# Four chained transformer blocks: attention buffers in four one-batch places, five threads of 1, 1, 2, 2 and 2 batches

## The chip, the cores and the metric

The kernel runs on one core of a Trainium2 chip. The metric is the device time of one execution in microseconds (us), the median of repeated runs. Everything is computed in 32-bit floats. The core's engines are TensorE (PE in the profile, with PEld for its weight loads), VectorE (DVE), ScalarE (ACT), GpSimd (POOL) and SyncE (SP), which here issues DMAs only.

## The reference

Eight batches of 128 tokens with 256 features (x) and a context of the same shape (ctx) pass through four blocks. Attention has 16 heads everywhere. Cut to what matters:

```python
# L0: heads of 16 features, key mask per batch
x = x + attn(ln(x) @ q_w, ctx @ k_w, ctx @ v_w, mask) @ cproj_w
x = x + gelu_tanh(ln(x) @ fc_w) @ proj_w              # 256 -> 1024 -> 256
# L1: keys and values from [ctx, x], so 256 keys; mask on the ctx half
y = attn(x @ q_w, [ctx, x] @ k_w, [ctx, x] @ v_w, mask) @ out_w + x
x = gelu_tanh(rmsnorm(y) @ mlp_w1) @ mlp_w2 + x
# L2: twice, with heads of 128 features and one learned key and value more
for i in (1, 2):
    x = x + attn(ln(x) @ wq, [ctx @ wk, bias_k], [ctx @ wv, bias_v]) @ wo   # 256 -> 2048 -> 256
x = x + gelu(ln(x) @ w_fc1) @ w_fc2
# L3: self-attention, cross-attention, MLP; the masks multiply and shift the scores
q, k, v = split(ln(x) @ w_qkv);  x = x + attn(q, k, v, ltor_mask) @ w_ao
x = x + attn(ln(x) @ w_q, *split(ctx @ w_kv), cross_mask) @ w_co
x = x + gelu_tanh(ln(x) @ w1) @ w2
```

Biases stand on every product, and `ln` has a scale and an offset. The batches do not depend on one another.

## The kernel before

**Threads.** `SIZES` (line 25) splits the eight batches into threads, `(2, 2, 2, 2)`. One thread takes its batches through all four blocks (`blocks`, line 1362). Each thread loads all weights itself through `loader` (line 510): pieces of 512 KB from HBM, up to 4 pieces held per thread and 11 in all (`NW, NWT`). A thread's loader and blocks start when the thread two before it has left block 1 (`front_done`) and the thread three before it has left the wide attention of block 2 (`wide_done`).

**The order of the work** is written by a planner (class `Plan`, line 77 and after) when the program is built. Every piece of work is a generator that asks for buffers (`Slots`), waits for events, and asks for an engine with an urgency. The planner keeps a clock, gives each engine the most urgent piece that is ready, and estimates what the piece lasts with `_weight`. The urgencies are the sum of a number for the kind of work (`U`) and one for the thread's stage (`LATE`). What comes out is a fixed order of instructions per engine; on the chip only data and buffers make an engine wait. Where TensorE has nothing to do[...], the planner issues a matmul of the identity as a filler (`idle_work`, line 397). DMAs are issued by SP in order, in the first microseconds by ACT too.

**Line 333** is where the wrapper of the engines issues every compute instruction, so nearly all rows of the profile name L333, and tile names tell them apart. `mm`, `tl` and `sc` are banks of PSUM: two banks for products, two for small things, and one tile of four banks for scores. `w` is a piece of weights, `hT` the normed activations transposed, `kb` a buffer for MLP activations and for keys and queries of the wide attention, `t` one for scores of the softmax.

**Products.** `proj` (line 541) gives feature-major results: a 128x128 piece of weights is the stationary operand, and the thread's tokens stream (256 columns for two batches). `back` (line 683) gives token-major results: 128 tokens are stationary and 256 columns of weights stream, batch by batch. Each f32 matmul of the program shows as two records in the trace, a transpose as one.

**Small-head attention** (`attention`, line 799) has two cores. `by_keys` (blocks 0 and 1) computes scores twice, once for the maxima, and exponentiates them with keys on the partitions. `by_pairs` (block 3) has queries on the partitions, multiplies and adds the mask on DVE and POOL, exponentiates on ACT, normalizes on POOL, and transposes. `attn_lock` lets two threads hold buffers for keys `k`, values `v`, queries `q`, result `attnT` and `mask`, each with room for two batches.

**Wide attention** (`wide_attention`, line 1163) goes through four groups of four heads, twice. `keys_values` (line 1172) makes a group's keys and values from the context alone, so it may run early: `AHEAD` names the groups that a thread makes before its block 0. The learned value's bias comes through two loads, `bv` and `bb`, and a subtraction on POOL (`value_bias`, line 1289); there are two buffers for `bv` and one for `bb`. `group` (line 1232) makes queries and scores, and `after_scores` (line 1302) the rest.

Of the kernel before, what the change touches and what calls it, by code (L numbers as in the profile page):

```python
# [18 lines left out]
P = 128  # L19
B = 8  # L20
D = 256
# [3 lines left out]
SIZES = (2, 2, 2, 2)  # L25
# [37 lines left out]
AHEAD = [[(1, 0), (1, 1)], [], [], []]  # L63
U = {'take': -0.44, 'taken': -1, 'norm': -0.47, 'mask': 0.26, 'k': 2.41, 'q': 1.79, 'v': 2.5, 'by key': 0.5, 'softmax': 2.46, 'weights': 1.63, 'pairs': 0.75, 'out': 1.79, 'mlp norm': 0.75, 'mlp 1': 4.29, 'mlp 2': 1.92, 'wide norm': -1, 'wide k': 3.49, 'wide q': 4.0, 'wide v': 4.43, 'wide s': 1.19, 'wide': -0.3, 'ahead': 4.34, 'load': -0.39}
LATE = [(1.69, 2.1, 2.22, -0.57, 1.75, 0.04, 2.53, 1.2, 4.53, 1.81), (12.77, 7.95, 10.47, 7.4, 1.7, -1, 8.48, 3.14, 7.46, 6.32), (3.27, 2.62, 3.89, 0.6, 2.14, -1, 4.58, 4.56, 5.62, 0.26), (0.03, 1.69, 0.31, 1.11, 0.24, 3.18, -0.81, -0.64, -0.7, 1.05)]
# [17 lines left out]
class Plan:  # L83
# [12 lines left out]
    def __init__(self):  # L96
        self.now = 0
        self.seq = 0
        self.events = []
        self.asked = []  # L100
        self.until = {e: 0 for e in self.SEEN}
        self.weight, self.shared, self.wrote = 0, False, []
        self.idle_work = None
        self.both_until = {"DVE": 0, "POOL": 0}
        self.clock = Clock()
        self.count = 0
        self.log = []
        self.table = None
        self.dma_until = 0
        self.live = {}  # L110
# [152 lines left out]
def _weight(eng, name, args, kw):  # L263
# [25 lines left out]
    if eng == "DVE":  # L289
# [6 lines left out]
        if n <= 8:  # L296
            return 68, False
# [40 lines left out]
class Engines:  # L338
    def __init__(self, nc, plan):
        self.tensor, self.vector = Engine(nc.tensor, plan, "PE"), Engine(nc.vector, plan, "DVE")  # L340
        self.scalar, self.gpsimd = Engine(nc.scalar, plan, "ACT"), Engine(nc.gpsimd, plan, "POOL")
        self.sync = nc.sync


def op(eng, f, lat=None, table=None):
    return ((eng, 480 if eng == "SP" else 0, f, lat, table),)
# [8 lines left out]
def four_blocks(ctx: ExitStack, tc: tile.TileContext, a: dict, out: bass.AP):  # L355
# [35 lines left out]
    attn_lock, x1_slots = Slots(2), Slots(2)  # L391
    row_slots, bv_slots, bb_slots, w_slots = Slots(2), Slots(2), Slots(1), Slots(NWT)

    def kb():
        return new(act, [P, 2 * P], "kb", bufs=20)

# [15 lines left out]
    def dma(f, kb_, early):  # L412

        yield op("SP", lambda: f(nc.sync)) + (op("ACT", lambda: f(nc.scalar)) if early else ())
# [38 lines left out]
    class Thread:  # L453
        def __init__(self, h, b0, nb):
# [10 lines left out]
            self.late = 0.0  # L465
            self.ahead = {}

# [5 lines left out]
    def weight_list():  # L473
# [22 lines left out]
        for i in (1, 2):  # L496
            for hg in range(4):
# [12 lines left out]
    def loader(T):  # L510
        names = list(weight_list())
        first = {f"l{i}{hg}{x}" for i, hg in AHEAD[T.h] for x in "kv"}
# [23 lines left out]
    def drop(T, n=1):  # L536
        plan.put(T.w_slots, n)
# [47 lines left out]
    def norm(T, src, e, w, b, adds, rows, hT, ready, row_done, urgency):  # L585
# [4 lines left out]
        else:  # L590
# [17 lines left out]
            def root():  # L608
# [11 lines left out]
                if b is not None:  # L620
                    nc.vector.tensor_tensor(z, mean, v, ALU.mult)

# [60 lines left out]
    def back(lhsT, n, w, x, row_in, then):  # L683
# [3 lines left out]
        def part(b, c0):  # L687
            def f(p):
                q = parts(p, nb, D)
                for c in range(c0, min(c0 + 4, n)):  # L690
                    nc.tensor.matmul(
                        q[:, b, :], lhsT=lhsT(c)[:, b * P : (b + 1) * P], rhs=w(c),
# [11 lines left out]
    def product(ops, take):  # L704
# [5 lines left out]
        return spawn(taken(p, take), U["taken"], Plan.SEEN["PE"])  # L710
# [6 lines left out]
    def mlp(T, name, src, e, w, b, b1, func, table, adds, to):  # L717
# [7 lines left out]
        def first():  # L725
            yield (kb_slots, NF)
            for m in range(0, NF, 2):
                hs = [kb(), kb()]
                hid.extend(hs)

                def take(p, m=m, hs=hs):
                    yield from each(*(op("ACT", lambda i=i: nc.scalar.activation(
                        hs[i][:, : T.nt], p[:, i * T.nt : (i + 1) * T.nt], func, bias=col(b1, m + i)), None, table)
                        for i in range(2)))
                hid_in.append((yield from product(
                    proj(T.w[f"{name}1{m // 4}"], hT, (m % 4, m % 4 + 1)), take)))
                if m % 4 == 2:
# [9 lines left out]
        def second():  # L747
            yield from product(*back(lambda c: hid[c], NF, lambda c: T.w[f"{name}2{c // 4}"][:, c % 4, :], to,
                                     row_in, lambda: plan.set(there)))
            drop(T, 2)  # L750
            plan.put(kb_slots, NF)
# [4 lines left out]
    def key_bias(mask, dst, hs, ks, ks_in, name, dtype, T, may_be_none):  # L756
# [5 lines left out]
        raw = mask[:, 0].rearrange("p b k -> p (b k)").bitcast(dtype)[:, : T.nt].rearrange("p (b k) -> p b k", b=nb)  # L762
        m = mask[:, 1]
        ms = new(act, [P, 2, nb], "ms", bufs=2)
        kss = new(act, [P, 2, NC, nb], "kss", bufs=2)
        yield spawn(load(raw, a[name][:, T.tokens].rearrange("o (b k) -> o b k", k=P).partition_broadcast(P), 64 * nb), -1)
        yield ks_in

        def minus():
            nc.vector.tensor_scalar(m, raw, 0.0, -BIG, ALU.is_equal, ALU.mult)  # L770
            some = new(act, [P, nb], "some", bufs=2)
# [5 lines left out]
            for e in range(2):  # L777
                nc.vector.tensor_scalar(hs[:, e], some, half[e], None, ALU.mult)
                nc.vector.tensor_scalar(ms[:, e], some, mask_row[e], None, ALU.mult)
                for c in range(NC):  # L780
                    nc.vector.tensor_scalar(kss[:, e, c], some, ks[:, e, c : c + 1], None, ALU.mult)

        yield op("DVE", minus)
        yield from each(*(
# [14 lines left out]
    def attention(T, name, norm, ns, own_keys, scale, qb, kb_, vb, mask_of, masks, to):  # L799
# [6 lines left out]
        yield (attn_lock, 1)  # L806
        hT, hT_in = yield from normed(T, *norm, U["norm"] + late)
        ready, row_in = T.ready, T.row_in
        mask = new(act, [P, 2, nb, P], "mask", bufs=2)
        hs = new(act, [P, 2, nb], "hs", bufs=2)  # L810
        ne = 2 if by_key else 1
        k = new(act, [P, 2, NC, nb, 2, P], "k", bufs=2)[:, :ne, :, :, :ns]
        v = new(act, [P, 2, nb, 8, 3, 16], "v", bufs=2)[:, :ns]
        q = new(act, [P, 2, NC, nt], "q", bufs=2)
        attnT = new(act, [P, NC, nt], "attnT", bufs=2)
# [64 lines left out]
        def queries():  # L880
            def take(p):
                yield from each(*(either(
                    lambda m=m, e=e: nc.scalar.activation(
                        q[:, e, m, :], p[:, m * nt : (m + 1) * nt], AF.Identity,
                        bias=qs[:, e, m : m + 1], scale=par[e]),
                    lambda m=m, e=e: nc.vector.tensor_scalar(
                        q[:, e, m, :], p[:, m * nt : (m + 1) * nt], par[e], qs[:, e, m : m + 1], ALU.mult, ALU.add),
# [17 lines left out]
        def out():  # L905
            yield from product(*back(lambda c: attnT[:, c, :], NC, lambda c: wo[:, c, :], to,
# [3 lines left out]
            plan.put(attn_lock)  # L910
# [5 lines left out]
    def by_keys(T, ns, scale, mask, masks, q, k, v, v_in, vb, attnT):  # L916
# [4 lines left out]
        def item(b, c0, n):  # L921
            tok = slice(b * P, (b + 1) * P)
# [5 lines left out]
            def by_query():  # L928
                for e in range(2):
                    for c in cs:  # L930
                        j = e * n + c - c0
                        for r in range(4):
                            part = slice(32 * r, 32 * r + 32)
                            nc.tensor.matmul(
                                s[:, r, j * nk : (j + 1) * nk], lhsT=q[part, e, c, tok],
# [25 lines left out]
            to = q[:, :, c0 : c0 + n, tok]  # L961
# [513 lines left out]
```

## Time and profile before

| | |
|---|---|
| median of 3 runs | 1197.38 us (1197.1 to 1198.49) |
| the profiled execution | 1198.46 us |
| its span, first to last instruction | 1196.7 us |
| TensorE busy | 1145.7 us, 8318 records |
| VectorE, ScalarE, GpSimd busy | 751.2, 574.1, 339.1 us |
| moved by DMA | 145.59 MB, mean 122 GB/s |
| matmuls of the identity (mm<-ident) | 92 records, 17.4 us |
| loads of activation tables on ACT | 50, 64.2 us |

How to read it: busy times are unions of an engine's instructions. Matmuls are pipelined; a record of a matmul reaches about 0.17 us into the next one, so the distance from one start to the next is the pace, not the length of a record. The rows of 40 digits cut the span into slices of 30 us. The chain of work that ended last goes back from the last instruction to what released it, step by step.

### The profile page before, as it was taken

What the parts mean: (1) busy time and instruction counts of PE and PEld (TensorE: products, weight loads), DVE (VectorE), ACT (ScalarE), POOL (GpSimd) and SP (SyncE); (2) the same over time, 40 slices, a digit from 0 to 9 for tenths busy, and PEclk for the clock granted to TensorE, in tenths of its full rate; (3) what the DMA queues carried; (4) which work ended last, traced back from release to release, by engine and by line L of the source; (5) the groups of instructions that cost most, each with busy time, mean ns of one, the idle gap of its engine ahead of it and who ended that gap; (6) DMA issues with size and microseconds to landing.
All of it is one profiled execution on the core that took longest, in us unless ns stands there. A gap on an engine that the chain in (4) does not pass through costs nothing.

```text
span 1196.7 us, 21922 instructions
## 1 busy us (share of the span) xinstructions
PE 1145.7 (96%) x8318; PEld 937.0 (78%) x8318; DVE 751.2 (63%) x1943; ACT 574.1 (48%) x1448; POOL 339.1 (28%) x392
## 2 busy tenths in 40 slices
PE   8899889999999999999999999999999999999888
PEld 7577668788887777787888897787887887877767
DVE  7755668744554867977872365626568456778872
ACT  4344544452433345675653243434436334686972
POOL 4021111112221210360611022211217212475870
PEclk9899999999999999999999999999999999999999
DMA  9423131336444324343324644543544543432120
GB/s 319 131 84 116 54 98 58 125 117 191 131 147 132 107 90 130 103 133 97 118 85 130 190 145 121 161 157 125 145 130 141 159 133 111 134 100 67 51 80 18
DMA packets 107321, 145.59 MB, mean 122 GB/s; under 512 B 6736, under 2 KB 66256, under 8 KB 107216
## 3 DMA queue, kind: packets, MB, share of 16 engines
q1 hardware_dynamic: 105984, 143.02, 38.3%
q8 instruction: 66, 1.08, 0.4%
q10 hardware_dynamic: 1232, 1.16, 0.3%
q14 instruction: 39, 0.32, 0.1%
HBM read 143.11 MB, written 1.05 MB: 120 GB/s over the span
## 4 chain that ended last, share of the span: by engine, by line
PE 78%; DVE 13%; ACT 5%; issue 1%; POOL 1%; DMA 0%; ACTq 0%; POOLq 0%; DVEq 0%
PE mm L333 57%; PE tl L333 17%; PE sc L333 5%; DVE t L333 2%; DVE mp L333 1%; DVE rz L333 1%; ACT t L333 1%; ACT pt L333 1%; DVE mn L333 1%; ACT q L333 1%; POOL t L333 1%; DVE ry L333 1%; DVE q L333 1%; ACT L333 1%; DVE rv L333 1%
## 5 line engine op out<-in xcount | busy, mean ns | idle before, releaser
L333 PE MATMUL mm<-hT,w 128*128 128x256 f32 x1216 | 286.7, 382 | 5.9 <-ACT kb L333 1.8
L333 PEld LDWEIGHTS mm<-hT,w 128*128 128x128 f32 x1216 | 223.7, 190 | 46.1 <-issue 6.4
L333 POOL TENSOR_TENSOR t<-t,sm 128x512 f32<-128x512 f32 x128 | 132.2, 1043 | 296.6 <-DVE sm L333 215.2
L333 PE MATMUL mm<-ctxT,w 128*128 128x256 f32 x608 | 144.0, 381 | 2.2 <-DVE k L333 2.1
L333 PE MATMUL mm<-w,ctxT 128*128 128x512 f32 (+1 forms) x352 | 143.8, 537 | 1.2 <-ACT k L333 0.7
L333 PEld LDWEIGHTS mm<-ctxT,w 128*128 128x128 f32 x608 | 111.5, 190 | 19.2 <-issue 4.2
L333 DVE TENSOR_TENSOR x<-mm,x 128x256 f32<-128x256 f32 (+1 forms) x96 | 49.0, 511 | 119.6 <-PE mm L333 118.9
L333 PE MATMUL mm<-w,at 128*128 128x256 f32 x512 | 120.4, 380 | 1.9 <-ACT kb L333 1.9
L333 PE MATMUL mm<-w,kb 128*128 128x256 f32 x512 | 117.5, 381 | 0.0
L333 POOL TENSOR_TENSOR x<-x,row 128x512 f32<-128x512 f32 x40 | 50.8, 1270 | 230.5 <-ACT xn L333 118.5
L333 PEld LDWEIGHTS mm<-w,at 128*128 128x128 f32 x512 | 94.8, 190 | 17.5 <-issue 2.6
L333 PEld LDWEIGHTS mm<-w,kb 128*128 128x128 f32 x512 | 95.3, 190 | 13.9 <-issue 1.1
L333 ACT ACTIVATE t<-t,mn 128x128 f32<-128x128 f32 x256 | 99.1, 390 | 11.6 <-DVE mn L333 10.3
L333 ACT ACTIVATE at<-tl,cols 128x128 f32<-128x128 f32 x224 | 64.0, 369 | 62.2 <-PE tl L333 61.9
L333 PEld LDWEIGHTS mm<-w,ctxT 128*128 128x128 f32 x352 | 63.4, 190 | 37.8 <-issue 31.4
L333 POOL TENSOR_TENSOR bv<-bv,bb 128x512 f32<-128x512 f32 x32 | 40.7, 1271 | 178.6 <-DMA bb<-in_L_bias_v 153.7
L333 POOL TENSOR_TENSOR t<-t,mask 128x512 f32<-128x512 f32 x64 | 79.8, 1273 | 26.3 <-DVE t L333 22.4
L333 PE MATMUL tl<-ident,t 128*128 128x128 f32 x512 | 75.6, 275 | 9.0 <-POOL t L333 4.0
L333 PEld LDWEIGHTS tl<-ident,t 128*128 128x128 f32 x512 | 60.3, 141 | 25.9 <-POOL t L333 12.9
L333 ACT ACTIVATE t<-t 128x516 f32<-128x516 f32 x64 | 40.5, 633 | 79.4 <-DVE t L333 79.1
L333 ACT ACTIVATE kb<-mm,cols 128x256 f32<-128x256 f32 x128 | 53.0, 472 | 52.0 <-PE mm L333 51.7
L333 DVE TENSOR_TENSOR vw<-mm,bv 128x512 f32<-128x512 f32 x64 | 43.7, 684 | 46.8 <-PE mm L333 46.6
(121 smaller groups left out, 1797.8 us busy)
## 6 DMA issues: line engine op xcount, KB each, us to landing
w<-in_L_wk SPq DMA_DIRECT2D x32, 512.0 KB, 3.7
w<-in_L_wv SPq DMA_DIRECT2D x32, 512.0 KB, 3.9
w<-in_L_wq SPq DMA_DIRECT2D x32, 512.0 KB, 3.7
w<-in_L_wo SPq DMA_DIRECT2D x32, 512.0 KB, 3.9
bv<-in_L_bv SPq DMA_DIRECT2D x32, 256.0 KB, 4.9
bb<-in_L_bias_v SPq DMA_DIRECT2D x32, 256.0 KB, 5.5
w<-in_L_mlp_w SPq DMA_DIRECT2D x16, 512.0 KB, 3.9
w<-in_L_w_fc SPq DMA_DIRECT2D x16, 512.0 KB, 4.3
```

What stands on the lines that cost most here:

```text
L333: return f(*args, **kw)
```

## The change

- `SIZES` becomes `(1, 1, 2, 2, 2)`: threads 0 and 1 have one batch, threads 2 to 4 have two. A thread starts when the thread three before it has left block 1 and the wide attention (`FRONTS, WIDES = 3, 3`), so three threads start at once.
- The buffers of the small attention are no longer two sets for two batches each, but shared tiles with four places of one batch (`k4`, `v4`, `q4`, `attnT4`, `mask4`). `take` gives a thread as many places as it has batches, and `give` returns them. The residual `x1` of block 1 gets four places too.
- One-batch threads put four head pieces into two buffers `kb` (`kbs_of`), in the MLP as well, and the first MLP product and the wide products work on four pieces at once where they had two.
- `AHEAD` names two groups for thread 0, as before, and one for thread 2. Early groups could also be kept in buffers `t`; no entry asks for it. The evacuation of early keys and values has an urgency of its own.
- `BY_BATCH = (4,)`: the last thread goes through block 3 as two parts of one batch that run beside each other and share weights; a piece is dropped when both parts are done with it.
- `key_bias` computes the mask before it waits for the key biases.
- The planner's numbers: `U` and `LATE` are new, and some costs that it works with (DMA issue, small DVE operations) changed.

```diff
-SIZES = (2, 2, 2, 2)
+SIZES = (1, 1, 2, 2, 2)
...
-AHEAD = [[(1, 0), (1, 1)], [], [], []]
+FRONTS, WIDES = 3, 3
+BY_BATCH = (4,)
+AHEAD = [[(1, 0), (1, 1)], [], [(1, 0)], [], []]
...
-    attn_lock, x1_slots = Slots(2), Slots(2)
+    attn_slots, x1_slots = Slots(4), Slots(4)
...
+    def kbs_of(n, nt):
+
+        per = 2 * P // nt
+        ts = [kb() for _ in range(n // per)]
+        return [ts[i // per][:, i % per * nt : (i % per + 1) * nt] for i in range(n)]
+
+    places, x1_places = [0, 1, 2, 3], [0, 1, 2, 3]
+    k4 = new(const, [P, 4, 2, NC, 2, P], "k")
+    v4 = new(const, [P, 4, 2, 8, 3, 16], "v")
+    q4 = new(const, [P, 4, 2, NC, P], "q")
+    attnT4 = new(const, [P, 4, NC, P], "attnT")
+    mask4 = new(const, [P, 4, 2, P], "mask")
+    x14 = new(const, [P, 4, D], "x1s")
+
+    def take(of, n):
+        got = [of.pop(0) for _ in range(n)]
+        return got, slice(got[0], got[-1] + 1, max(1, got[-1] - got[0]))
...
-        yield (attn_lock, 1)
+        yield (attn_slots, nb)
+        got, at = take(places, nb)
...
-            for m in range(0, 4, 2):
-                yield (kb_slots, 2)
-                two = [kb(), kb()]
+            step = 4 // nb
+            for m in range(0, 4, step):
...
-        if h > 1:
-            yield front_done[h - 2]
-        if h > 2:
-            yield wide_done[h - 3]
+        if h >= FRONTS:
+            yield front_done[h - FRONTS]
+        if h >= WIDES:
+            yield wide_done[h - WIDES]
...
+        T.parts = [Part(T, b) for b in range(nb)] if h in BY_BATCH else []
+        for e in [spawn(last_block(p, LATE[h][7 + 3 * i : 10 + 3 * i]), 0) for i, p in enumerate(T.parts)] or [
+                spawn(last_block(T, LATE[h][7:10]), 0)]:
+            yield e
+
+    def last_block(T, late):
+        x, nb = T.x, T.nb
+        T.late = late[0]
```

## The prediction, made before the changed kernel was run

> **What bounds the kernel now.** I read the page first (busy shares, the 40 slices, the chain), then busy time by stretch, then TensorE's groups, then the timeline for the true pace of its matmuls.
>
> ```profile
> PE 1145.7 (96%) x8318; PEld 937.0 (78%) x8318; DVE 751.2 (63%) x1943; ACT 574.1 (48%) x1448; POOL 339.1 (28%) x392
> ...
> PE   8899889999999999999999999999999999999888
> ...
> DMA  9423131336444324343324644543544543432120
> ...
> PE 78%; DVE 13%; ACT 5%; issue 1%; POOL 1%; DMA 0%; ACTq 0%; POOLq 0%; DVEq 0%
> ```
>
> TensorE is the bound: 78% of the chain that ended last, no other engine near it. But a matmul's record overlaps the next one, so 96% busy is not 96% used. The pace must come from starts:
>
> ```profile
> 276.17 10.52 PE L333 MATMUL mm<-w,kb 128*128 128x256 f32 x48
> 286.53 0.60 PE L333 MATMUL tl<-ident,x 128*128 128x128 f32 x4
> 286.97 1.89 PE L333 MATMUL mm<-hT,w 128*128 128x256 f32 x8
> ...
> 293.88 1.95 PE L333 MATMUL tl<-kb,kb 128*128 128x128 f32 x16
> 295.66 1.88 PE L333 MATMUL mm<-w,ctxT 128*128 128x512 f32 x4
> ```
>
> 48 matmuls of 256 columns take 286.53 - 276.17 = 10.36 us, 215.7 ns each; 16 of 128 columns take 295.66 - 293.88 = 1.78 us, 111.5 ns each; 4 transposes take 0.44 us, 109 each. Likewise 429 for 512 columns, and 29 (57 for 256 columns) for the records that run four row groups side by side. All 8318 records at these paces, fillers (below) at nothing, are 1077 us of work. The span is 1196.7, so about **120 us are lost** in gaps and slow stretches, and only those can be won. The same sum by stretch of the trace: 0 to 240 us holds 186 us of work (54 lost), 240 to 390 148.5 (1.5), 390 to 600 189 (21), 600 to 1020 412 (8), 1020 to 1170 119 (31); the rest is the last 27 us. So the loss lies at the front (blocks 0 and 1 of the first threads), at the end (block 3 of the last ones), some in the middle. The 16-head wide attention of block 2 fills TensorE wherever it is there.
>
> ```profile
> 0.00:240.00 240.00, 217.50 (x2027) 174.54 (x2028) 165.79 (x461) 106.95 (x189) 41.27 (x73) 0.98 0.38 123
> 240.00:390.00 150.00, 149.62 (x771) 124.00 (x770) 68.52 (x168) 57.52 (x136) 32.07 (x42) 1.00 0.46 145
> 390.00:600.00 210.00, 202.75 (x1827) 164.55 (x1826) 166.85 (x431) 122.77 (x282) 67.11 (x73) 1.00 0.37 111
> 600.00:1020.00 420.00, 417.01 (x2363) 343.14 (x2362) 228.01 (x555) 168.41 (x423) 95.71 (x105) 1.00 0.45 138
> 1020.00:1170.00 150.00, 136.14 (x1233) 111.18 (x1232) 116.31 (x310) 113.25 (x410) 101.70 (x99) 1.00 0.26 82
> ```
>
> (Stretch, length, busy of PE, PEld, DVE, ACT, POOL, granted clock, DMA share, GB/s.) DVE is at 69% to 79% in the lossy stretches, never full: they lose time to chains (scores, maxima, exponentials, weighting, norm), not to one engine's throughput. More independent chains are the cure.
>
> **The change, part by part.** The sum is made against the profiled execution: 1198.46 us, 1.8 outside its span and 1.1 above the median 1197.38.
>
> *One batch in each of threads 0 and 1, three threads in the front.* The four batches of the front are the same, in three chains instead of two, the first two half as long. Comparing the order of instructions that both programs issue: at the paces above the first wide scores come after 104 us of TensorE work instead of 135. Up to 150 us of work (203 us of time) the kernel before loses 51 us: 28 in the first 90 and 23 in the next 60. The fillers (matmuls of the identity that the planner puts in where TensorE would idle) stand there 16 and 16; after the change 19 and none. Two ways to size the gain: fillers in proportion, 51 x 13/32 = 21 us; or loss per work, 44 us lost in the 135 before the first wide scores, so 0.33 x 104 = 34 after, and 6 more up to 150, makes 40 and a gain of 11. The first 90 us (19 fillers against 16) I leave as they are; the next 60, with 16 us of wide work where there were 4, should lose what stretches with that much lose, 2 to 3 us in each 30, so 6 instead of 23. I take **-17**; bounds -28 and 0.
>
> *Columns.* 1040 of the records now stream 128 columns instead of 520 with 256 (matmuls of ctxT or hT with w). Same columns, twice the instructions: 1040 x (111.5 - 107.9) = **+4 us**. A rule speaks against me here: the Trainium skill, "TensorE: Matmul & The Clock Gate", section "Back-to-back issue gap", says that in a stream of weight loads and matmuls 128 columns sustain about 81 ns where the isolated figure is about 56: 25 ns each for exposed weight loads, 26 us by estimate. The row decides: tl<-kb,kb has a new 128x128 weight for every 128 columns, in the same f32, and still runs at 111.5. So +4; bounds 1 and 26.
>
> *Weights.* Every thread loads all weights itself, so five threads load 180 MB instead of 145. By the order of loads against that of matmuls, the 60 us of work from 150 on ask for 17.9 MB, 298 GB/s; the first 30 us of work ask for 16.2 MB instead of 10.6.
>
> ```profile
> 15.00:20.00 5.00, 4.89 (x50) 3.74 (x48) 4.24 (x18) 3.40 (x8) 0.00 (x0) 1.00 1.07 368
> 25.00:30.00 5.00, 4.37 (x49) 3.18 (x47) 4.86 (x9) 2.17 (x7) 2.65 (x3) 1.00 0.94 322
> ```
>
> The queue moved 319 GB/s over the first 30 us, up to 368 in 5. So 17.9 MB need 56 us at 319, just under the 60. Much of the 5.6 MB more at the start is early keys and the third thread, which TensorE doesn't need yet. It is close enough to cost some late weights: **+3**; bounds 0 and 20. Every DMA waits on SP in order: 102 more of them at 0.4 us are 41 us of SP over the run, hidden, but a load held by its buffer holds all behind it.
>
> *Early keys.* Thread 0 keeps its two early groups, half as large; thread 2 gets one. They are useful work where the front has gaps, and are counted in the -17. No entry of AHEAD names the home "t", so that new path doesn't run.
>
> *Places.* Keys, values, queries, masks move into shared four-place tiles. The waits on DVE, ACT and POOL of instructions that write them hardly grow in number, so I charge nothing; a false wait would show as a rival below.
>
> *Small work.* DVE gets 243 more instructions (1919 to 2162), half of them the ten-step root chains (0.16 to 0.27 us a step) of 12 more norms; ACT 10 more table loads (12.8 us) and 81 others; POOL 8 more bias subtractions (10 us). TensorE's work hides them: DVE at 63% rises by 243 x 0.17 = 41 us to 66%. Without that cover 10 us of them would show. **0**; bounds -0 and +10.
>
> *The end.* Thread 4 goes through block 3 batch by batch, in two chains that share weights, beside thread 3. After the last wide scores 141 us of work are left instead of 151; at the 0.21 lost per us before (31 in 150) this wins 2. But fillers there are 16 instead of 14, by proportion +4.5, and the four-step softmax with POOL at 68% (101.7 of 150) is crowded into fewer us. After the last attention projection 21 us of dense MLP work stand in both orders. **+1**; bounds -10 and +10. The last store is 128 KB, not 256: -0.4.
>
> Sum: -17 + 4 + 3 + 0 + 1 - 0.4 = -9.4. Profiled 1189, median 1197.4 - 9.4 = **1188**.
>
> **The rivals.** *More is won.* Two half-long chains also shorten the first 90 us (a third of 28, -9), and the middle (21 lost at 390 to 600) gives up a third too (-7): 1172. For it: three chains run from the start. Against: 19 fillers where there were 16, and one in the middle in both orders.
>
> *Nothing comes of it.* The front's gain is 0 to 8 because the by-key attention still goes through one four-bank score tile for all threads, and the other terms eat it: 1197. For it: waits of PE on DVE's maxima lead the chain's early part ("DVE mp" pieces of 2.3 us). Against: the wide work that now covers them uses other banks.
>
> *Slower: the loads bind.* Place: the one-batch wide groups of threads 0 and 1. Price: 17.9 MB at a delivered rate r take 17.9/r instead of 60 us. It turns the 9.4 won into more than 2.4 lost when the wait passes 11.8 us: r under 249 GB/s. At 230 it is 18 us late, 1206. For it: loads wait for 11 buffers, in SP's order, so the queue can't be kept full; the learned-bias buffer bb is single:
>
> ```profile
> L420 SPq DMA_DIRECT2D bb<-in_L_bias_v x32: 340/382/1117, 15.9 to 990.6; - x32
> L333 POOL TENSOR_TENSOR bv<-bv,bb x32: 1261/1269/1323, 21.9 to 996.2; 128x512 f32<-128x512 f32 x32
> ...
> DMA to landing us min/median/max: 4.3/5.5/7.6
> ```
>
> Landing 5.5 and 1.27 to subtract are 6.8 us a group; a one-batch group has 9.1 us of TensorE work (two-batch 18.2). Against: it fits, even at 7.6.
>
> A false wait between places of one shared tile would look like "nothing comes of it"; I put it there.
>
> **How the numbers follow.** As summed 0.57 (own range 1179 to 1194.9), more won 0.13, nothing 0.10, loads bind 0.20. A measurement here can't tell less than 0.2% (2.4 us) from no change; faster is the first two, 0.70, same 0.10, slower 0.20. The range leaves out half of each outer case: 1171 to 1205.
>
> **What would show it.** Right: in the first 200 us of the new trace TensorE's loss by start-to-start pace is near 34 instead of 51, wide scores begin before 150 us of time, matmuls of 128 columns keep 111 to 113 ns. DMA share at 0.8 to 0.9 somewhere in 180 to 270 us, with few waits of TensorE behind w. The last 170 us lose about 31 as before. Wrong: 128-column matmuls at 130 ns or more; gaps of several us before mm<-w,ctxT or mm<-ctxT,w with the DMA full; or an end that loses 40 with TensorE waiting for POOL's t.

## The result, and the profile after

The changed kernel takes 1195.24 us, median of 12 runs (1190.83 to 1200.48), beside 1198.33 us for the kernel before (12 runs, 1196.78 to 1200.76): ratio 0.9976, 95% interval 0.9962 to 0.9989. Run again on another occasion it took 1194.95 beside 1197.88, ratio 0.9969 (0.9956 to 0.9981). It is 3.1 us faster, where 9.4 were forecast. The profiled execution took 1194.78 us, its span is 1193.0 (before: 1198.46 and 1196.7). Among the twelve executions the time goes with the granted clock of TensorE, from 1190.83 us at a mean of 0.997 to 1200.48 at 0.989.

The page of the changed kernel: busy time by engine, the rows of 40 slices of 30 us, and the shares of the chain.

```profile
PE 1150.5 (96%) x8816; PEld 956.5 (80%) x8816; DVE 798.8 (67%) x2186; ACT 596.3 (50%) x1538; POOL 360.4 (30%) x446
...
PE   7999999999999999999999999999999999988978
...
PEclk8999999999999999999999999999999999998999
DMA  9754567787645554435334534446443564351120
...
PE 79%; DVE 11%; ACT 5%; DMA 2%; issue 1%; POOL 0%; SPq 0%; ACTq 0%; POOLq 0%; DVEq 0%
```

TensorE is the bound as before. The PE digits hint at the front: the second to sixth slices went from 8, 9, 9, 8, 8 to 9 throughout, and the first from 8 to 7. The DMA row has risen to 7 and 8 around 180 to 300 us, where the one-batch threads ask for their wide weights.

Busy time by stretch, changed kernel (stretch, length, busy of PE, PEld, DVE, ACT, POOL, granted clock, DMA share, GB/s):

```profile
0.00:240.00 240.00, 223.62 (x2133) 187.37 (x2134) 170.34 (x522) 115.19 (x239) 51.03 (x94) 0.98 0.66 204
240.00:390.00 150.00, 147.70 (x1059) 124.73 (x1057) 102.56 (x271) 73.28 (x182) 43.07 (x53) 1.00 0.65 203
390.00:600.00 210.00, 205.90 (x1694) 170.42 (x1694) 149.12 (x407) 114.33 (x252) 59.60 (x78) 1.00 0.48 144
600.00:1020.00 420.00, 418.36 (x2645) 343.32 (x2644) 258.31 (x645) 186.62 (x492) 118.68 (x127) 1.00 0.46 140
1020.00:1170.00 150.00, 135.18 (x1170) 112.76 (x1169) 114.93 (x332) 100.90 (x357) 87.25 (x93) 0.98 0.28 82
```

TensorE is busy 6 us more than before in the first stretch, 3 more in the third. A finer account is needed: busy is not used, and the same piece of work stands at another time. So I cut both traces by **TensorE's work done** (the paces of the prediction, start to start; fillers count as nothing), and call the rest of each distance loss:

| us of work | before: lost | after: lost | difference |
|---|---|---|---|
| 0 to 30 | 11.1 | 17.7 | +6.6 |
| 30 to 90 | 17.3 | 16.0 | -1.3 |
| 90 to 150 | 22.9 | 5.9 | **-17.0** |
| 150 to 930 | 31.6 | 34.5 | +2.9 |
| 930 to the end | 31.4 | 33.5 | +2.1 |
| more work in the records | | | +3.8 |
| after the last TensorE record | 4.0 | 3.3 | -0.7 |
| sum | | | **-3.7** |

-3.7 is the difference of the two spans up to rounding. The +3.8 is the count of the records at the paces of the prediction, so it tests that pace no further than the rows under "Columns" below do. Inside 150 to 930 two shifts nearly cancel: 150 to 330 loses 6.1 more (small-head attention of later threads stands there now: 128 records tl<-pt,v where there were 64), 330 to 570 loses 5.0 less.

### The profile page after: what moved, and what is told of

Read it like the earlier page. It is cut to its first block, busy times and chain, and to the rows that moved or that the text cites. A ratio compares the mean times of both kernels' runs of the same rounds, so it can differ in the third digit from the quotient of the medians.

```text
span 1193.0 us, 23579 instructions
## 1 busy us (share of the span) xinstructions
PE 1150.5 (96%) x8816; PEld 956.5 (80%) x8816; DVE 798.8 (67%) x2186; ACT 596.3 (50%) x1538; POOL 360.4 (30%) x446
## 4 chain that ended last, share of the span: by engine, by line
PE 79%; DVE 11%; ACT 5%; DMA 2%; issue 1%; POOL 0%; SPq 0%; ACTq 0%; POOLq 0%; DVEq 0%
PE mm L335 57%; PE tl L335 17%; PE sc L335 5%; DVE rz L335 2%; ACT kb L335 1%; DVE t L335 1%; DMA w<-in_L_wk 1%; DMA bb<-in_L_bias_v 1%; ACT t L335 1%; DVE mn L335 1%; ACT q L335 1%; DVE ry L335 1%; ACT pt L335 1%; DVE kb L335 1%; DVE q L335 1%
## 5 line engine op out<-in xcount | busy, mean ns | idle before, releaser
L335 PE MATMUL mm<-hT,w 128*128 128x256 f32 (+1 forms) x1576 | 292.4, 335 | 12.0 <-ACT kb L335 2.5
L335 PEld LDWEIGHTS mm<-hT,w 128*128 128x128 f32 x1576 | 242.8, 191 | 43.5 <-issue 8.0
L335 PE MATMUL mm<-ctxT,w 128*128 128x256 f32 (+1 forms) x768 | 148.7, 342 | 1.7 <-DVE x L335 0.8
L335 PEld LDWEIGHTS mm<-ctxT,w 128*128 128x128 f32 x768 | 121.7, 194 | 16.5 <-issue 3.0
L335 POOL TENSOR_TENSOR x<-x,row 128x256 f32<-128x256 f32 (+1 forms) x48 | 48.0, 999 | 232.7 <-ACT xn L335 108.3
L335 POOL TENSOR_TENSOR bv<-bv,bb 128x512 f32<-128x512 f32 x40 | 50.8, 1271 | 153.2 <-DMA bb<-in_L_bias_v 137.0
L335 ACT ACTIVATE at<-tl,cols 128x128 f32<-128x128 f32 x212 | 60.4, 371 | 46.5 <-PE tl L335 46.2
L335 ACT ACTIVATE kb<-mm,cols 128x256 f32<-128x256 f32 (+1 forms) x168 | 59.5, 422 | 43.5 <-PE mm L335 43.2
```

The source lines that it names most:

```text
L335: return f(*args, **kw)
```

## The experiments

The changed kernel once more, with the first experiments on one chip:

> The changed kernel once more, on the chip that the three next ones run on, so that they can be read against it. Every theory expects about 3 us less than the kernel before, a ratio of 0.9975.

Measured 1194.95 us. In the profile the first 60 us of work lose 28.2 us (28.0 in the first one): the start is what repeats.

### Where the start went

In the first 30 us of work, what does TensorE wait for? The chain of the kernel before and of the changed one, first pieces in order of time (start us, length us, what):

```profile
2.26 5.76 DMA w<-in_L_cproj_w
8.04 0.43 ACTq L333
8.65 0.44 issue
9.09 0.59 ACT xn L333
```

```profile
0.73 2.86 DMA x<-in_x
3.60 8.07 DMA w<-in_L_wk
11.70 0.38 ACTq L335
12.07 0.05 issue
12.12 0.61 ACT xn L335
```

In the built program every load takes one of eight semaphores in rotation, so it is issued only when the load eight places before it has landed. ACT issues the first x, then thread 1's x and, in the changed kernel, thread 1's context, ahead of its first norm `xn` in program order. The context waits there for the early keys' weights `wk` (0.5 MB), and the first norm behind it: 12.12 us, where the kernel before starts its first norm at 8.58 (the chain shows its second record, at 9.09). That was my first theory.

**Thread 1's context with thread 0's** (one load of 256 tokens; ACT's load of it is gone; compute in the same order):

```diff
-            rows = (load(T.x, ...), load(T.ctx, a["ctxT"]...[:, :, T.tokens], ...))
+            T_c = (load(ctxT[:, :, : 2 * P], a["ctxT"]...[:, :, : 2 * P], 128, early) if h == 0
+                   else dma(planned_only, 128, early) if h == 1 else load(T.ctx, ...))
+            rows = (T_x, T_c)
```

> Thread 1's context comes with thread 0's (one load of 256 tokens, as the kernel before had it), so that ScalarE has one DMA less ahead of its first norm (xn). The order of everything else stays. Theory 'ScalarE's DMA holds the first norm': in the changed kernel the DMA of ctxT waits until the load of wk has landed at 11.67 us and the first xn starts at 12.12; without it xn starts soon after the DMA of x (issued at 9.61), at about 10.1, and the clock drop of 10 to 20 us shrinks: 2 to 4 us faster than the changed kernel. Theory 'the start is bound by the loads' (three threads ask for 16.2 MB in the first 30 us of work): the same bytes come, so within 1 us of the changed kernel.

Measured 1194.71 us, ratio 0.9972 (0.996 to 0.9983), against 1194.95 for the changed kernel on the same chip. The first norm did start at 8.48 us instead of 12.12, and next to nothing came of it: the first 60 us of work lose 26.9. As the whole cause the theory fell. TensorE was let go earlier and then stood before the next late thing, thread 1's x, for which its statistics `st` wait here:

```profile
14.69 0.43 DVE L335 BATCH_NORM_STATS2 st<-x 128x6 f32<-128x256 f32 x1 [4.17 <-DMA x<-in_x]
```

**Thread 1's x and context with thread 0's** (also x of both threads in one tile and one load):

```diff
+    x01 = new(const, [P, 2, D], "x01")
...
-            self.x = new(const, [P, nb, D], f"x{h}")
+            self.x = x01[:, h : h + 1, :] if h < 2 else new(const, [P, nb, D], f"x{h}")
```

> Thread 1's x and context both come with thread 0's, so no DMA stands ahead of the first xn on ScalarE but thread 0's own four. Theory 'ScalarE's DMA holds the first norm': xn starts at 6.5 to 8 us instead of 12.12, the first matmuls of the queries some 4 us earlier, no low clock between 10 and 20 us: 4 to 7 us faster than the changed kernel, 1188 to 1191. Theory 'the start is bound by the loads': PE waits for w instead, within 1.5 us of the changed kernel.

Measured **1190.95 us**, ratio 0.9935 (0.9923 to 0.9948), 4.0 us less than the changed kernel beside it; the first 60 us of work lose 21.7 us instead of 28.2, and each later stretch of 30 us agrees with the changed kernel's beside it within 1.2 us. How thread 1 starts shows why. Timeline rows of the kernel before, of the changed one, and of this one: the issue of thread 1's x, its statistics `st` (the first use of x) and its first transposes `tl`.

```profile
8.04 0.43 ACTq L333 DMA_DIRECT2D x<-in_x  x1
15.28 0.75 DVE L333 BATCH_NORM_STATS2 st<-x 128x6 f32<-128x256 f32 x2 [0.92 <-DMA x<-in_x]
19.60 0.29 PE L333 MATMUL tl<-ident,xn 128*128 128x128 f32 x1
```

```profile
9.61 0.35 ACTq L335 DMA_DIRECT2D x<-in_x  x1
14.32 0.42 DVE L335 BATCH_NORM_STATS2 st<-x 128x6 f32<-128x256 f32 x1
19.17 0.38 PE L335 MATMUL tl<-ident,xn 128*128 128x128 f32 x2
```

```profile
10.41 0.42 DVE L335 BATCH_NORM_STATS2 st<-x 128x6 f32<-128x256 f32 x1
14.44 0.38 PE L335 MATMUL tl<-ident,xn 128*128 128x128 f32 x2
```

Before and after, thread 1 reaches TensorE at the same time, 19.6 and 19.2 us. But by then TensorE had done 9.99 us of work before the change and 4.65 after it (sum of the paces up to that record): **thread 0 with one batch has half the work with which to cover thread 1's loads**. With x and context there earlier, thread 1 comes after the same 4.65 us of work at 14.44. In the changed kernel two late things lie on each other: `st` shows no wait for x there, because thread 0's own norm, held by the context's DMA, was as late.

The gap brings a second cost. Stretches of 5 us, changed kernel, then the one with x and context together (columns as above):

```profile
10.00:15.00 5.00, 3.54 (x15) 2.79 (x16) 2.31 (x14) 2.35 (x6) 0.45 (x1) 0.56 0.93 306
15.00:20.00 5.00, 3.71 (x25) 3.41 (x25) 3.57 (x20) 2.32 (x8) 0.00 (x0) 0.76 0.98 318
```

```profile
10.00:15.00 5.00, 3.58 (x30) 3.42 (x31) 4.43 (x23) 3.12 (x10) 0.36 (x1) 1.00 0.85 294
15.00:20.00 5.00, 4.51 (x55) 3.58 (x53) 4.18 (x11) 2.82 (x9) 1.84 (x4) 1.00 1.08 364
```

TensorE is as busy from 10 to 15 us in both, but in the first with a granted clock of 0.56, and of 0.76 in the next 5 us. As an estimate from these rows, 3.54 x 0.44 + 3.71 x 0.24 = 2.4 us of the loss are records that ran slower. Against the kernel before this is hardly an extra cost: it has 1.00 in both stretches, but its own stretch of low clock from 30 to 60 us, where the changed kernel has 1.00:

```profile
30.00:60.00 30.00, 25.02 (x282) 17.56 (x280) 21.32 (x46) 9.37 (x11) 0.09 (x2) 0.89 0.44 130
```

By the same estimate that is 25.02 x 0.11 = 2.8 us. This profile of the changed kernel has one more, 0.94 from 60 to 90 us (27.23 x 0.06 = 1.6). So the low clock accounts for part of what x and context together win over the changed kernel, but, by these estimates, for only 2.4 + 1.6 - 2.8 = 1.2 us of what the changed start loses to the kernel before.

**The same edit in the kernel before** (x of threads 0 and 1 in one load) tells whether late x costs there too:

```diff
-            rows = (load(T.x, ..., 128 * T.nb, early),
+            T_x = load(x01, a["x"][0:4]..., 256, early) if h == 0 else dma(planned_only, 256, early) if h == 1 else ...
```

> The kernel before with thread 1's x in one load with thread 0's (512 KB), the order of all else kept. In both kernels thread 1's x lands at 14.3 to 15.3 us and its first transposes start at 19.2 to 19.6; up to there TensorE has done 10.0 us of work in the kernel before and 4.7 in the changed one. Theory 'half the batches are half the cover': two batches of thread 0 cover most of thread 1's start here, so 0 to 2 us faster than before, less than half of what the same edit gives in the changed kernel (4). Theory 'a late x costs both the same': 3 to 5 us faster than before.

Measured 1199.96 us, ratio 1.0004 (0.9996 to 1.0012). Nothing: thread 1's statistics start at 14.25 us instead of 15.28, but its transposes stay at 19.57 us with 9.99 us of work done. With two batches in thread 0, x is not what holds thread 1. The context was not moved here, so this run is the counterpart of the next one, not of the one with both.

**Thread 1's x alone with thread 0's, the context where it was:**

```diff
+            T_c = load(T.ctx, a["ctxT"]...[:, :, T.tokens], 128 * T.nb, early)
```

> The changed kernel with thread 1's x in one load with thread 0's, its context as in the changed kernel. Theory 'thread 1's x is what is late' (moving the context alone won nothing): 1190.5 to 1192.5, 3 to 5 us faster than the changed kernel, as with both moved. Theory 'ScalarE's DMA holds the first norm': the context's DMA still stands ahead of the first xn, so less than 2 us faster.

Measured 1192.41 us, ratio 0.9953 (0.994 to 0.9966). That is 2.5 us under the changed kernel's 1194.95 of another occasion (3.4 when each is taken against the kernel before beside it, 1.9 by the ratios): between the two expectations. Thread 1's transposes come at 14.16, but then its `mm<-ctxT,w` at 16.30 waits 1.71 us for the context, the granted clock is 0.55 from 15 to 20 us, and thread 2's statistics come at 25.25 us instead of 20.80 in the run with both. The profiled execution (1194.75 us, above its median) loses 26.5 in the first 60 us of work, so the trace shows only some 1.5 us won; the medians decide. Either load alone leaves TensorE standing before the other.

**Later x and context of threads 3 and 4,** on top of x and context together, to leave the first 60 us to what is needed:

```diff
+            if plan.now > 60000:
+                while later:
+                    later.pop(0)(tc.nc.sync)
```

> As e1_both (thread 1's x and context come with thread 0's), and the x and context of threads 3 and 4, 1 MB that nothing reads before 250 us, are issued after 60 us instead of at 20 to 31. Theory 'the loads bind the first 35 us' (DMA moves 319 to 367 GB/s there in e1_both): 1 MB is 3 us of it, so 1 to 3 us faster than e1_both, a ratio to the kernel before of 0.991 to 0.9927. Theory 'the start was the first norm alone and is mended': as e1_both, 0.9935.

Measured 1189.63 us, ratio 0.9924 (0.9912 to 0.9937). The intervals overlap with those of the run without it; the start loses 23.1 against 21.7. Not told apart. Both versions beat both kernels.

### The four-place tiles

**Only the tiles:** the changed program with the old sizes, numbers and costs.

```diff
-SIZES = (1, 1, 2, 2, 2)
+SIZES = (2, 2, 2, 2)
...
-FRONTS, WIDES = 3, 3
-BY_BATCH = (4,)
-AHEAD = [[(1, 0), (1, 1)], [], [(1, 0)], [], []]
+FRONTS, WIDES = 2, 3
+BY_BATCH = ()
+AHEAD = [[(1, 0), (1, 1)], [], [], []]
```

> The changed program with the old sizes, numbers and costs: 2, 2, 2, 2, two threads in the front, no part by batch. Its order is that of the kernel before; what is left of the change is that keys, values, queries, masks and results lie in shared four-place tiles. Theory 'the places cost nothing' (the prediction): within 1.5 us of the kernel before. Theory 'places bring false waits or slower access': 3 us or more slower, in the stretches with small-head attention.

Measured 1203.58 us, ratio 1.0042 (1.0027 to 1.0056): slower, where I had charged nothing. All stretches after the first 30 us of work lose the same as in the kernel before; the first loses 17.5 instead of 11.1. One load (`bb`) had moved up in SP's order, by the 0.3 that the change adds to the urgency of each further early group. So once more without it, with the loads in the order of before:

```diff
-            T.ahead[i, hg] = keys_values(T, i, hg, LATE[h][0] + U["ahead"] + 0.3 * n, ...)
+            T.ahead[i, hg] = keys_values(T, i, hg, LATE[h][0] + U["ahead"], ...)
```

> As e4_places, but the second early group has no later urgency, so the loads keep the order of the kernel before (in e4_places one 256 KB load of a bias, bb, had moved from 18th to 10th place on SP). Only the four-place tiles and what goes with them are left of the change. Theory 'the order of the first loads made e4_places slow': within 1.5 us of the kernel before. Theory 'the places themselves are slow': 4 us slower again.

Measured 1202.5 us, ratio 1.0042 (1.0025 to 1.0059); first stretch 15.1. Still slower, with the loads in the order of before. What I saw to differ is one load: the byte mask of block 0 for two batches is one row of 256 bytes on each partition before, and two pieces of 128 bytes in the four-place tile. So the mask's load was put back, as whole rows into a tile of its own:

```diff
-        raw = mask[:, 0].bitcast(dtype)[:, :, :P]
+        raw = new(act, [P, nb * P // 4], "raw", bufs=2).bitcast(dtype)... if name == "mask_b" else mask[:, 0]...
```

> The old sizes, numbers and costs with the four-place tiles, with the order of loads of the kernel before (the e4b kernel, 1202.5 us, ratio 1.0042), and one thing put back: the byte mask of block 0 is loaded into a tile of its own, 256 bytes in a row on each partition, where the four-place tile takes it as two pieces of 128 bytes. Everything is computed, and every instruction stands in the same order. Theory 'small pieces hold up the first loads': with the pieces gone the mask lands at about 8.0 us again (10.6 with the pieces), thread 1's x is issued at 8.0 instead of 10.9, the first 30 us of TensorE work lose 11 to 12 us instead of 15.1, and the time is 1197 to 1200, within 0.15% of before. Theory 'the places themselves' (false waits on the shared tiles, or where they lie in memory): nothing moves, 1201 to 1204, first bin 14.5 to 16 us.

Measured 1199.32 us beside 1199.52, ratio 0.9996 (0.9987 to 1.0005): the cost is gone. Timeline rows with the pieces, then with whole rows: SP's second mask load and ACT's load of thread 1's x, both of which wait for loads of the first eight.

```profile
10.63 0.38 SPq L448 DMA_DIRECT2D mask<-in_mask_b  x1
10.63 0.29 DVE L335 TENSOR_SCALAR mask<-mask 128x256 f32<-128x256 uint8 x1 [2.78 <-DMA mask<-in_mask_b]
10.91 0.37 ACTq L335 DMA_DIRECT2D x<-in_x  x1
```

```profile
8.03 0.68 SPq L448 DMA_DIRECT2D raw<-in_mask_b  x1
8.54 0.38 ACTq L335 DMA_DIRECT2D x<-in_x  x1
```

The second row of the first fence says that the mask landed at 10.63; thread 0's mask load is issued at 2.24 us in both runs, so it did not wait for its tile. With 128 pieces more in a load of 32 KB, it and the load issued beside it (`cproj_w`, for whose semaphore thread 1's x waits) landed some 2.5 us later. The profiled execution lost 13.9 in its first stretch, more than expected; it was the slowest of its 14 runs (1203.11 us), so the medians decide here.

**Does that hold in the changed kernel?** There threads 0 and 1 have one piece a partition each. Both masks in one load of 256-byte rows:

```diff
+        joint = name == "mask_b" and T.h < 2
+        if joint:
+            raw = raw01[:, T.h : T.h + 1]
...
+        yield spawn(dma(planned_only, 64, False) if joint and T.h else load(raw01, a[name][:, : 2 * P]..., 64) if joint else load(raw, ...), -1)
```

> The changed kernel with one thing altered: the byte masks of threads 0 and 1 come in one load, 256 bytes in a row on each partition, into a tile of its own, instead of two loads of 128 bytes a partition each; thread 1's mask load is gone from SP's queue (its planned slot stays, so all compute stands in the same order). Everything is computed. Theory 'small pieces and the place in the rotation hold up the first loads here too': thread 1's x is issued near 8.0 us instead of 9.6, thread 0's first norm near 9 instead of 12.1, and the first 60 us of TensorE work lose 2 to 4 us less than the 28 of the changed kernel: 1191 to 1193. Theory 'one batch is too little cover for thread 1's x': x still lands at 14 us, the loss stays at 26 to 29, and the time at 1194 to 1196.

Measured 1196.72 us, ratio 0.9979 (0.9972 to 0.9986): as the changed kernel. Thread 0's norm starts at 12.04, thread 1's statistics at 15.84, and the first 60 us of work lose 29.1. The masks don't hold up the start of the changed kernel.

### Do the loads bind?

**More to load:** two spare loads of 64 KB beside each wide piece of threads 0 and 1, 8.4 MB in all, into two tiles that nothing reads.

```diff
+            if T.h < 2 and name[0] == "l" and name[1] in "12":
+                for i in range(2):
+                    tc.nc.sync.dma_start(out=spare[i], in_=pieces[0][1][:, i, :P])
```

> With each wide weight piece of threads 0 and 1 two more loads of 64 KB go to a tile that nothing reads: 128 x 64 KB x... 8.4 MB more in all, a quarter more in the stretch that asks for 17.9 MB in 60 us of work. Theory 'the loads have room there' (the trace of the changed kernel shows no wait of PE for w after the first 160 us): within 2 us of the changed kernel. Theory 'the loads bind' (the rival of the prediction): 22 MB in 60 us are past the 319 GB/s of the first 30 us, 8 us or more slower.

Measured 1217.22 us, ratio 1.0155 (1.0139 to 1.0171). The stretches from 150 to 240 us of work lose 27.5 us instead of 3.8, and I read it at first as loads with no room left. The waits of SP's queue from 200 to 300 us say otherwise (us in total, times, longest):

```profile
SPq L574 <- DMA spare<-in_L_wk: 16.8, 6, 4.4
SPq L574 <- DMA spare<-in_L_wo: 12.9, 7, 4.7
SPq L574 <- DMA spare<-in_L_wq: 11.9, 7, 5.7
SPq L574 <- DMA spare<-in_L_wv: 8.4, 7, 3.5
```

Each spare load writes a tile that the spare load two before it wrote, and waits until that has landed; all weights wait behind it on SP, 50 us in 100. The queue delivered less than in the changed kernel (241 against 274 GB/s from 240 to 270 us), not more. The experiment measured its own wait. So again, each load of 128 KB to a place of its own:

```diff
+    spare = tc.nc.dram_tensor("spare", [64, P, 2, P], F32, kind="Internal").ap()
...
+                tc.nc.sync.dma_start(out=spare[next(spares)], in_=pieces[0][1][:, :2, :P])
```

> The changed kernel with one spare load of 128 KB beside each piece of wide weights of threads 0 and 1 except the early keys and values (60 loads, 7.9 MB), each to a place of its own in HBM that nothing reads. Everything is computed. In the run with two spare tiles each spare load had to wait for the one two before it, and the queue behind it too; here none waits for another, only for one of the eight in flight. Theory 'the delivered rate binds': the 60 us of work from 150 on ask for some 22 MB, over what was delivered, the DMA share there goes above 0.9, TensorE waits for w, and the time is 1210 or more. Theory 'the queue waited for the spare tiles': the loads have room, stretches 150 to 240 lose 2 to 8 us in all more than in the changed kernel, and the time is 1195 to 1204.

Measured 1196.0 us, ratio 0.9973 (0.9965 to 0.9981): 7.9 MB more cost nothing. Stretches of this run:

```profile
210.00:240.00 30.00, 29.56 (x238) 26.35 (x237) 20.63 (x61) 12.25 (x32) 7.74 (x10) 1.00 0.97 284
240.00:270.00 30.00, 28.57 (x175) 23.84 (x175) 12.94 (x28) 14.63 (x36) 6.28 (x7) 1.00 0.94 303
```

```profile
PE mm L335 <- DMA w<-in_L_wq: 0.8, 1, 0.8
```

A share of 0.97 for 30 us and 303 GB/s over the next 30, with one wait of TensorE for a load, 0.8 us, in the 200 us from 100 to 300. The loads are ahead of need there; what cost time in the run before was a queue that stood still.

### Early keys and the end

**No early keys for thread 2** (a new plan, with the numbers of the changed kernel):

```diff
-AHEAD = [[(1, 0), (1, 1)], [], [(1, 0)], [], []]
+AHEAD = [[(1, 0), (1, 1)], [], [], [], []]
```

> The changed kernel without thread 2's early keys and values (1.5 MB of loads less in the first 40 us). The planner orders all anew. Theory 'the loads bind the start': the first 60 us of TensorE work lose 24 us or less instead of 28, though the planner puts 27 fillers there instead of 15. Theory 'the early keys fill the front': they lose 31 or more, 3 to 8 us slower.

Measured 1225.3 us, ratio 1.0224 (1.0207 to 1.0241). The first 60 us of work lose 35.3 instead of 28.0, but 450 to 540 also lose 18.8 instead of 7.0: the plan is another one to the end and its numbers fit none of it. It fits the view that these keys fill the front; their worth can't be read from a plan that differs to the end.

**The last block 3 whole** instead of batch by batch (also planned anew):

```diff
-BY_BATCH = (4,)
+BY_BATCH = ()
```

> The changed kernel without the part by batch: thread 4 goes through block 3 with both batches as one. The planner orders the end anew, without urgencies found for it; it puts 39 fillers in the last 90 us of TensorE work where the changed kernel has 16. Theory 'by batch helps the end': the loss after 930 us of TensorE work grows from 33 to 38 to 50 us, so 5 to 17 us slower than the changed kernel. Theory 'by batch makes the end worse' (the loss there was 31 before the change): 2 to 6 us faster.

Measured 1204.33 us (1199.71 to 1208.29), ratio 1.0043 (1.003 to 1.0057). Up to 990 us of work all stretches but the start are as in the changed kernel within 1 us; from there to the end it loses 38.1 instead of 30.7. So going batch by batch is worth 7 us in the trace and 9 in the medians, with numbers not fitted to the whole form, which may be part of the difference.

## Why the prediction was right or wrong

The direction was right, and so was the mechanism of the gain (-17 where -17.0 came), but one term put at nothing was not: -9.4 forecast, -3.1 in the medians, -3.7 between the profiles. Term by term:

| term of the sum | forecast | measured | |
|---|---|---|---|
| front, first 90 us of work "left as they are" | 0 | **+5.3** | the step that failed |
| front, next 60 us | -17 | -17.0 | right |
| columns | +4 | +3.8 | right, by the measured pace |
| weights | +3 | 0 where it was looked for | no wait from 100 to 300 us; 7.9 MB more cost nothing |
| places | 0 | 0 here | right by the sizes, see below |
| small work | 0 | within the +2.9 of 150 to 930 | not separated |
| end | +1 | +2.1 | within its bounds, but see below |
| last store | -0.4 | -0.7 | right |

**The step that failed** is "The first 90 us (19 fillers against 16) I leave as they are". I followed chains of compute and asked what more chains cover; I did not ask what covers the first *loads*. Thread 1's statistics start at 14.32 us where they started at 15.28, nearly the same time, and a thread 0 of half the size has half the work before thread 1's (4.65 us instead of 9.99). "Which TensorE doesn't need yet" was the second half of the mistake: the early keys' weights `wk` were not needed yet, but thread 1's context stood behind them in the rotation, and thread 0's norm behind the context. And one load of weights was late, in these 90 us and not in the 60 from 150 on (the kernel before waits for none in its first 60 us):

```profile
PE mm L335 <- DMA w<-in_L_v_w: 2.0, 1, 2.0
```

That x and context come late is shown: the run with both together gives the loss back, 21.7 us in the first 60 us of work where the kernel before loses 23.0, and 1190.95 us. That it matters because thread 0 has one batch rests on the two runs that move x alone: 2.5 us won after the change, nothing before it. Moving the context too in the kernel before was not tried. The size has a spread: four executions with the changed kernel's start (two of it, one with block 3 whole, one with spare loads to HBM) lose 28.0, 28.2, 25.0 and 29.1 in these 60 us. The one that loses 25.0 has a granted clock of 1.00 throughout the first 90 us of its trace, as the run with both has; the 3.3 us between these two are, as an estimate, the waits without the clock.

The prediction had a way to size this step and did not use it. At the end it scales the loss by the fillers; here that gives 28.4 x 19/16 = 33.7, which is what was measured. One agreement does not make it a rule: at the end it gave +4.5 where +2.1 came.

**Next 60 us.** Sized by what stretches with as much wide work lose, 6 instead of 23: measured 5.9 instead of 22.9. But of the two cruder ways for the whole front, gains of 21 and 11, the second was right to the microsecond: it forecast 40 us lost up to 150 us of work, and 33.7 + 5.9 = 39.6 are. That is luck as far as the runs show: the rule knows nothing of loads, and with x and context moved the same order loses 34.2 up to there.

**Columns.** The pace of 128-column records of hT and ctxT with w, timeline of the changed kernel:

```profile
161.48 1.95 PE L335 MATMUL mm<-ctxT,w 128*128 128x128 f32 x16
...
205.82 3.74 PE L335 MATMUL mm<-hT,w 128*128 128x128 f32 x32
```

A record reaches 0.17 us into the next, so (3.74 - 0.17) / 32 = 111.6 ns each. The 25 ns each that the rule cited in the prediction would have added aren't there.

**Weights.** From 100 to 300 us no wait of TensorE for a load is listed at all. The 319 GB/s of the first 30 us was the right row to lean on; the +3 was caution. That it nearly cancels the +2.9 of 150 to 930, for which the sum had put nothing, is luck. The rival "loads bind" was wrong about its place and its price: loads were late at the start, one at a time, not by the delivered rate at 150 us. Its other half, a load held on SP that holds all behind it, is what the run with two spare tiles showed by accident: 22 us.

**Places.** Charged nothing for false waits, and none was found. What they do cost, some 4 us with two-batch threads at the start, comes from the load of one mask, whose layout I had not looked at; with one-batch threads in front it doesn't arise.

**The end.** The +2.1 hides a stretch of low clock, 0.94 where the kernel before has 1.00:

```profile
1030.00:1090.00 60.00, 53.63 (x403) 45.35 (x402) 42.47 (x133) 33.32 (x105) 27.83 (x33) 0.94 0.38 112
```

As an estimate 53.63 x 0.06 = 3.2 us of slower records: at full clock the end would have lost about 1 us less than before. The prediction had no term for the clock, and what lets it fall there was not looked into.

**The rivals.** "Nothing comes of it" (1197) was nearest in time, for the wrong reason: its front gains 0 to 8, where the 60 us from 90 on gained 17 and the start took 5.3 of them. "More is won" counted on a shorter first 90 us, the opposite of what came.

## What to carry to other kernels

When work is cut into smaller pieces so that more chains run side by side, the first piece covers less of the loads that the second one waits for: count the bound engine's work before each first use of a load, and compare it with the time at which that load lands. Bring what the first pieces need together in early loads, all of it: here x alone or the context alone left TensorE standing before the other. Keep loads that wait out of a compute engine's queue. An experiment that adds a load must not make it wait for its own buffer, or it measures that.

## What the runs showed of the hardware that I had not expected

- After the waits at the start, the granted clock of TensorE was 0.56 from 10 to 15 us and 0.76 from 15 to 20 in the changed kernel, 1.00 in the one with x and context together. The kernel before has such a stretch later, 0.89 over 30 to 60 us, and the changed kernel a second one at its end, 0.94 over 1030 to 1090. So what a change does to the clock has to be counted over the whole span and not in one place.
- 128 pieces more (256 of 128 bytes for 128 of 256) in a load of 32 KB moved its landing, and that of the load beside it, by 2.5 us and the time by 0.4%.
- The loads ran at a share of 0.97 for 30 us and at 303 GB/s for the next 30 without TensorE waiting for them more than once.
